# A graph layer on one core: 23 instead of 16 edge tiles whose rows SyncE fetches by byte address, a later range check, and another order of the last two groups

## The chip, the cores and the metric

The kernel runs on 1 core of a Trainium2 chip. The metric is the device time of one execution in microseconds. The median of three runs before the change is 1509.13 us (1508.41 to 1510.37).

## The reference

A message-passing layer over 6250 nodes and 200,000 edges, sorted by destination, followed by a residual and a layer norm over 64 features:

```python
w = silu(edge_attr @ W1 + b1) @ W2 + b2                        # 200000 x 9
h_src = features[src]                                          # one row of 64 per edge
msg = einsum('ef,em,fmg->eg', h_src, edge_sh * w, W_tp)
agg = segment_sum(msg, dst, num_segments=N) / sqrt(AVG_DEG)
emb = silu(c_noise[:, None] @ Wn1 + bn1) @ Wn2 + bn2
gamma, beta = split(emb, 2, axis=-1)
x = layernorm(x + agg * (1.0 + gamma) + beta)
```

## The kernel before

The edges are cut into 1563 tiles of 128, and 16 tiles make a group: 98 groups (`NBLK`), 0 to 97, the last with 11 tiles. The step `i` of the main loop works on several groups at once, and the order in which each engine gets its work is written out by hand (`tc.manual_schedule()`): an engine's instructions stand in its queue as the code emits them.

The rows `x[src]` of a group come into the tile `hs[g]` in three ways:
- `gather(g)` (L91): GpSimd's indirect DMAs, one per tile, issued six groups ahead (`AHEAD`) into seven buffers.
- `pick(g, t)` (L477): TensorE multiplies one-hot matrices `hot_k` (made by VectorE, in `hots`) with the whole of `x`, which lies in SBUF in two parts (`xs`), 14 products per tile into `px`; VectorE selects and sums the rows (`xm`, L486, and the reduction, L488). `picked(g)` says how many tiles of a group: four, three where `g % 4 == 0`, and three in group 97.
- `load_rows(g, e0)` (L101, L106): in the 16 groups of `SPG` (7, 13, ..., 97) SyncE fetches the rows of the group's first tile, each with a small DMA of its own. It loads up to 8 row numbers from `src_r` into registers, and each row's address is worked out from the register. `SPR` = 22 rows are issued per step, over six steps.

`src_r` is filled in the setup by one DMA of 2048 single words (L280).

SyncE's queue also holds the loads of edge attributes (`ea`, `sh`; one pair of groups every second step), of the keys for the picks (`kr`), of node values (`cb`), and the stores of the output.

In step `i` TensorE has, in this order: the first pick of group `i + 1` with small products for finished nodes among it (`nodes`), `hidden(i + 2)` (the first layer on edges, L405), `second(i + 1)` (its second layer into the PSUM tile `p2`, L422), `windows(i)` (L510: the rows of group `i` times the edge weights, 16 tiles, into `pz`; ScalarE copies the result to `zt`), in odd steps `project(i // 2)` (L550, with `W_tp`), and the other picks of group `i + 1`, with the transposes of `weights(i + 1)` in the first of them. `place` adds a pair of groups into node windows, `bring` turns finished nodes back, and `finish` and `finish_nodes` do the residual and the norm; the store is issued at the top of the next step.

`reach(k)`, in steps 3, 4 and 5, checks that the edges of each group lie in the range of nodes that the fast path takes: two reductions over 1568 columns on VectorE, then the limits (`bad`), a product on TensorE that counts (`p_bad`, L335), and the flag. It comes behind `hots(i + 2, 2, Q)` on VectorE and ahead of `hidden` on TensorE. `p_bad` and `p2` take turns in one PSUM buffer (tag `s`). At the end every engine reads the flag, and would run `general_path` if it were not zero.

Step 96 and what follows the loop are written out for the last groups: `windows(96)`, the picks of group 97 with `project(48)` and `place(48)` among them, `bring` of nodes 46 and 47, `windows(97)`, `project(49)`, and the last nodes.

Of the kernel before, what the change touches and what calls it, by code (L numbers as in the profile page):

```python
# [6 lines left out]

F32 = mybir.dt.float32
I32 = mybir.dt.int32
F16 = mybir.dt.float16  # L10
# [17 lines left out]
LB = 2  # L28
Q = 4
J = 7  # L30
SPG = range(7, NBLK, 6)
SPR = 22
EPS = 1e-5

KH = 8
# [9 lines left out]
def pair(q):  # L45

    return [g for g in (2 * q - 1, 2 * q) if 0 <= g < NBLK]


def picked(g):  # L50

    return Q - (g % 4 == 0 or g == NBLK - 1)


def tiles(g):
# [4 lines left out]
def gnn_resnorm_kernel(ctx: ExitStack, tc: tile.TileContext, x, src, dst, dst_row, ea, sh, cn,  # L60
# [18 lines left out]
    with ExitStack() as fast:  # L79
# [16 lines left out]
        src_r = keep.tile([len(SPG), P], I32)  # L96

        def load_rows(g, e0):
            for e in range(e0, min(e0 + SPR, P), 8):
                n = min(8, min(e0 + SPR, P) - e)  # L100
                _, vs = nc.values_load_multi_w_load_instructions(  # L101
                    src_r[SPG.index(g):SPG.index(g) + 1, e:e + n], engines=[mybir.EngineType.SP],
                    min_val=0, max_val=NPAD - 1,
                    skip_runtime_bounds_check_because="src is below N, as for the gathers")
                for k in range(n):
                    nc.sync.dma_start(hs[g][e + k:e + k + 1, 0, :], x[bass.ds(vs[k], 1), :])  # L106

        ident = keep.tile([P, P], F32)
        ident2 = keep.tile([P, F], F32)
# [11 lines left out]
        nid = keep.tile([P, NBLK], F32)  # L121
        first_f = keep.tile([KB, NBLK], F32)
        bad = keep.tile([P, 4], F32)
        ext = keep.tile([P, 4], F32)
        C = NBLK * Q
        jl = keep.tile([P, C], F32)
# [8 lines left out]
        def setup(temp):  # L135
# [143 lines left out]
            with nc.allow_non_contiguous_dma(reason="2048 words, once"):  # L279
                nc.sync.dma_start(src_r, src[:, SPG[0] * KB:NBLK * KB:6 * KB].rearrange("p g -> g p"))  # L280
            first_t = temp.tile([NBLK, KB], F32)
            nc.scalar.copy(first_t, first_i)
            p_f = psum.tile([KB, NBLK], F32, tag="s", name="p_f")
# [37 lines left out]
        def reach(k):  # L321

            if k < 2:
                nc.vector.tensor_reduce(ext[:, k:k + 1], rel, AX.X, (ALU.max, ALU.min)[k])
                return
            at = late.tile([KB, NBLK], F32, tag="at", name="at", bufs=1)
            nc.vector.tensor_sub(at, first_f, lo[0:KB])
            nc.vector.memset(bad, 0.0)
            for i, op in enumerate((ALU.max, ALU.min)):
                nc.vector.tensor_reduce(ext[0:KB, 2 + i:3 + i], at, AX.X, op)  # L330
            for i, (n, lim, op) in enumerate(((P, W - 0.5, ALU.is_gt), (P, -0.5, ALU.is_lt),
                                              (KB, 2 * P - W + 0.5, ALU.is_gt), (KB, -0.5, ALU.is_lt))):
                nc.vector.tensor_scalar(bad[0:n, i:i + 1], ext[0:n, i:i + 1], lim, None, op0=op)
            p_bad = psum.tile([1, 4], F32, tag="s", name="p_bad")
            nc.tensor.matmul(p_bad, nf[:, 1:2], bad, start=True, stop=True)  # L335
# [21 lines left out]

        stores = []

        def finish(j0, j1, sums):  # L360
            y = late.tile([P, j1 - j0, F], F32, tag="y", name=f"y{j0}")
            o = finish_nodes(nc, late, eps, sums, y, gam[:, j0:j1, :], xb[:, j0:j1, :], j0)
            stores.append(lambda: nc.sync.dma_start(out_v[:, j0:j1, :], o))


        ea_t, sh_t, oh_t, kr_t, st, a, zs = {}, {}, {}, {}, {}, {}, {}
# [126 lines left out]
                nc.vector.memset(z[:, :, tiles(g):, :], 0.0)  # L493
            return z

        def windows(g):

            nk = tiles(g)
            hsg, ag = hs.pop(g), a.pop(g)
            z = zs[g] if g in zs else sums(g)  # L500


            end = g == NBLK - 1
            for k0 in reversed(range(0, nk, ZT)) if end else range(0, nk, ZT):
                n = min(ZT, nk - k0)
                pz = [psum.tile([P, ZT // 2, M, W], F32, tag="pz", name=f"pz{g}_{k0}", bufs=2)]
                pz.append(psum.tile([P, ZT // 2, M, W], F32, tag="px", name=f"pz{g}_{k0}_", bufs=2) if end else pz[0])
                for k in range(n):
                    v = k % 2
                    mm = nc.tensor.matmul(pz[v][v * F:(v + 1) * F, k // 2].rearrange("p m w -> p (m w)"),  # L510
                                          hsg[:, k0 + k, :], ag[:, k0 + k].rearrange("p m w -> p (m w)"),
                                          start=True, stop=True)
                    if k0 + k == 0:

                        for d in hs_dma.pop(g)[(g not in SPG):]:
                            tc.add_manual_dep(mm.ins, d.ins.name, mybir.DependencyInfo(
                                mybir.DependencyClass.Sync, mybir.DependencyReason.DATA), reason="rows of the group")
                for v in range(2):
                    for h in range(2):
                        (nc.vector.tensor_copy if end and v else nc.scalar.copy)(  # L520
                            z[h * F:(h + 1) * F, 0:5 - h, k0 + v:k0 + n:2, :].rearrange("p m k w -> p k m w"),
                            pz[v][v * F:(v + 1) * F, 0:(n + 1 - v) // 2, h:M:2, :])

# [2 lines left out]
        def halves(q, pr):  # L526

            n = len(pair(q))
            r[q] = work.tile([KW, 2, 2, F], F32R, tag="r", name=f"r{q}")
            nc.scalar.copy(r[q][:, 0:n, 0], pr)  # L530
            nc.vector.tensor_sub(r[q][:, 0:n, 1], pr, r[q][:, 0:n, 0].bitcast(F32))
            for g in pair(q):
                hot[g] = work.tile([KW, 2 * P], F32R, tag="c", name=f"c{g}")
                nc.vector.tensor_scalar(hot[g], nf[0:KW], nid[0:KW, g:g + 1], None, op0=ALU.is_equal)

# [40 lines left out]

            return [lambda k=k: part(k) for k in range(len(gs))]

        def bring(j0, j1, py):


            def part(j):
                nc.tensor.matmul(py[:, j - j0], yt.pop(j), ident2, start=True, stop=True)
                if j == j1 - 1:
                    finish(j0, j1, py[:, 0:j1 - j0])

            return [lambda j=j: part(j) for j in range(j0, j1)]

# [18 lines left out]
        with tc.manual_schedule(), tc.tile_pool(name="temp", bufs=1) as temp:  # L607
            setup(temp)

            for i in range(NBLK):  # L610
# [26 lines left out]
                if i + 1 < NBLK:  # L637
                    second(i + 1)
                if i < NBLK - 1:
                    windows(i)  # L640
                turn = project(i // 2) if i % 2 == 1 and i < NBLK - 1 else []
                if i % 4 == 1 and i - 1 < NJ:
                    gate_hidden(i - 1)
                if i + 1 < NBLK:
                    pick(i + 1, 1, [weights(i + 1), turn])
                if i == NBLK - 2:
                    sums(i + 1)
                    turn = project(i // 2)
                    ps = psum.tile([P, 2 * P], F32, tag="s", name="ps_l")
                    pick(i + 1, 2, [turn])  # L650
                    more = place(i // 2, ps)
                    if picked(i + 1) < Q:
                        for f in more:
                            f()
                        more = []
                    pick(i + 1, 3, [more])
                    continue
                for t in range(2, Q):
                    pick(i + 1, t)
            for f in bring(NJ - 3, NJ - 1, psum.tile([P, FB, F], F32, tag="s", name="py_l")):  # L660
                f()
            windows(NBLK - 1)
# [15 lines left out]
def finish_nodes(nc, work, eps, sums, y, gam, xb, tag):  # L678
# [12 lines left out]
    nc.scalar.activation(var, var, AF.Sqrt, bias=eps, scale=1.0 / F)  # L691
    nc.vector.reciprocal(var, var)
    o = work.tile([P, n, F], F32, tag="o", name=f"o{tag}")
    nc.vector.tensor_mul(o, y, var.unsqueeze(2).to_broadcast([P, n, F]))
    return o


def general_path(tc, dram, x, dst_row, ea, sh, src_i, dst_i, w1bd, b1c, w2bd, b2r, wtc,
# [3 lines left out]
    with ExitStack() as ctx:  # L702
# [109 lines left out]
        for j0 in range(0, NJ, JC):  # L812
# [7 lines left out]
            o = finish_nodes(nc, work, eps, a[0], a[0], gam[:, js, :], xb[:, js, :], f"g{j0}")  # L820
            nc.sync.dma_start(out_v[:, js, :], o)


# [47 lines left out]
```

## Time and profile before

| | |
|---|---|
| median of three runs | 1509.13 us (1508.41 to 1510.37) |
| profiled execution | 1511.72 us, span 1509.5 us |
| mean granted TensorE clock | 0.985 |
| TensorE products | 1450.0 us busy, 96% |
| VectorE | 1149.6 us busy, 76% |
| GpSimd | 1124.0 us busy, 74% |
| ScalarE | 514.4 us busy, 34% |
| rows fetched by SyncE | 2048 DMAs of 256 bytes |
| gathers by GpSimd | 1181 |

The span runs from the first to the last instruction of the profiled execution. A line of the groups names the source line, the engine, the operation, output and inputs, the count, then busy time and mean duration in ns, then the engine's idle time before these instructions and what ended it. A line of the waits has total time, count and the longest in us. A line of the timeline has start, duration, engine, line and operation, and in brackets the idle time before it. PE is TensorE, DVE is VectorE, ACT is ScalarE, POOL is GpSimd, SP is SyncE; a "q" behind a name means the engine's queue.

### The profile page before, as it was taken

How to read it: one execution, taken by the hardware profiler on the slowest of the kernel's cores; microseconds unless marked ns; L12 is line 12 of the kernel's file. 1: busy time of each engine (PE TensorE's matmuls, PEld its weight loads, DVE VectorE, ACT ScalarE, POOL GpSimd, SP SyncE). 2: the span in 40 equal slices, each digit the busy share in tenths (PEclk: the TensorE clock that was granted, in tenths of full speed). 3: DMA queues.
4: the chain of work that ended last, by engine and by line, in shares of the span. 5: the costliest groups of instructions: out<-in, count | busy, mean ns of one | idle time of the engine just before them, and what ended most of it. 6: DMA issues, size and time to landing. Idle time of an engine off the chain costs nothing.

```text
span 1509.5 us, 34713 instructions
## 1 busy us (share of the span) xinstructions
PE 1450.0 (96%) x10969; PEld 1206.6 (80%) x10969; DVE 1149.6 (76%) x2043; ACT 514.4 (34%) x1321; POOL 1124.0 (74%) x1190
## 2 busy tenths in 40 slices
PE   5898999999999999999999999999999999999995
PEld 3687888887888888887888888888888888888784
DVE  6776777878777778787787777777787886877773
ACT  3322333423332424333333324233243342333331
POOL 7777777777777777777777777777777777777773
PEclk8899999999999999999999999999999999999997
DMA  5422222222222222222222222222222222222210
GB/s 166 95 74 63 55 59 71 61 61 72 58 63 55 75 53 66 57 72 58 60 72 54 60 54 72 54 61 70 55 62 53 72 56 58 73 54 60 59 42 17
DMA packets 90953, 96.34 MB, mean 64 GB/s; under 512 B 37224, under 2 KB 51770, under 8 KB 90762
## 3 DMA queue, kind: packets, MB, share of 16 engines
q1 hardware_dynamic: 52394, 53.66, 12.4%
q0 software_dynamic: 37792, 38.77, 11.6%
q8 instruction: 89, 1.46, 0.4%
q10 hardware_dynamic: 576, 1.61, 0.3%
q14 instruction: 102, 0.84, 0.2%
HBM read 92.22 MB, written 1.73 MB: 62 GB/s over the span
## 4 chain that ended last, share of the span: by engine, by line
PE 66%; POOL 17%; issue 7%; DVE 4%; DMA 3%; ACT 2%; SPq 0%; POOLq 0%; DVEq 0%; ACTq 0%
PE px L477 50%; POOL hs L91 17%; PE pz L510 5%; PE p L405 4%; DMA hs<-in_x_dram,src_i 3%; PE pt L550 3%; PE p L422 2%; PE p L432 1%; ACT L413 1%; ACT st L413 1%; PE ps L566 1%; DVE xm L486 1%; PE ps L596 1%; DVE hs L488 0%; DVE y L686 0%
## 5 line engine op out<-in xcount | busy, mean ns | idle before, releaser
L91 POOL DMA_INDIRECT hs<-in_x_dram,src_i x1181 | 1122.7, 951 | 362.0 <-issue 328.5
L477 PE MATMUL px<-xs,hot_k 128*128 128x448 f32 x5124 | 1124.7, 373 | 2.7 <-ACT xs L235 1.3
L477 PEld LDWEIGHTS px<-xs,hot_k 128*128 128x128 f32 x5124 | 926.7, 189 | 87.1 <-DVE xs L236 3.5
L486 DVE SCALAR_TENSOR_TENSOR xm<-li,jl,px 128x448 f32<-128x448 f32 x366 | 247.5, 676 | 221.8 <-PE px L477 221.6
L462 DVE TENSOR_TENSOR hot_k<-pk,nk 128x896 fp32r<-128x896 f32 x366 | 381.7, 1081 | 2.9 <-PE pk L221 2.9
L413 ACT ACTIVATE st<-p,b1c 128x1024 f32<-128x1024 f32 x98 | 109.2, 1114 | 401.0 <-PE p L405 400.7
L488 DVE TENSOR_REDUCE hs<-xm 128x64 f32<-128x448 f32 x366 | 226.9, 620 | 12.6
L520 ACT COPY ztw<-pz 64x140 f32<-64x140 f32 (+1 forms) x780 | 209.1, 268 | 14.6 <-PE pz L510 5.8
L510 PEld LDWEIGHTS pz<-a,hs 128*64 128x64 f32 x3116 | 100.5, 139 | 48.2 <-issue 46.9
L510 PE MATMUL pz<-a,hs 128*64 128x63 f32 x3116 | 113.8, 226 | 7.4 <-DMA hs<-in_x_dram,src_i 6.2
L444 DVE TENSOR_TENSOR a<-oh,p 128x1008 f32<-128x1008 f32 x98 | 117.9, 1203 | 3.3
L405 PE MATMUL p<-ea,w1bd 64*128 64x512 f32 x392 | 112.5, 651 | 0.0
L572 ACT COPY carry<-ps 128x128 f32<-128x128 f32 x48 | 12.8, 266 | 274.1 <-PE ps L566 274.1
L438 DVE TENSOR_TENSOR p<-p,sh 128x72 f32<-128x72 f32 x196 | 46.9, 240 | 69.7 <-PE p L432 39.6
L422 PEld LDWEIGHTS p<-st,w2p 128*32 128x32 f32 x784 | 15.8, 108 | 86.8 <-issue 44.6
L691 ACT ACTIVATE var<-var,eps 128x2 f32<-128x2 f32 (+1 forms) x25 | 7.4, 296 | 208.3 <-DVE var L690 208.3
L422 PE MATMUL p<-st,w2p 128*32 128x256 f32 x784 | 63.4, 395 | 12.2 <-DVE xb L354 7.6
L550 PE MATMUL pt<-ztw,wtc 128*64 128x112 f32 x960 | 55.9, 263 | 2.8 <-ACT st L413 2.8
L456 ACT CAST pk<-kr 128x512 f32<-128x512 f16 (+1 forms) x96 | 54.0, 562 | 1.7 <-DMA kr<-kd 1.7
L432 PE MATMUL p<-ident,p2s 128*128 128x128 f32 x196 | 53.6, 273 | 0.0
L405 PEld LDWEIGHTS p<-ea,w1bd 64*128 64x128 f32 x392 | 29.9, 187 | 29.0 <-issue 27.2
L550 PEld LDWEIGHTS pt<-ztw,wtc 128*64 128x64 f32 x960 | 47.1, 138 | 4.8 <-ACT st L413 4.5
(133 smaller groups left out, 525.8 us busy)
## 6 DMA issues: line engine op xcount, KB each, us to landing
hs<-in_x_dram SPq DMA_DIRECT2D x2048, 0.2 KB
ea<-in_ea_dram SPq DMA_DIRECT2D x48, 512.0 KB
hs<-in_x_dram,src_i POOLq DMA_INDIRECT x1181
kr<-kd SPq DMA_DIRECT2D x48, 256.0 KB
sh<-in_sh_dram SPq DMA_DIRECT2D x49, 144.0 KB
cb<-cn_d SPq DMA_DIRECT2D x12, 128.0 KB
out_dram<-o SPq DMA_DIRECT2D x24, 64.0 KB
dst_i<-in_dst_dram SPq DMA_DIRECT2D x1, 768.0 KB
```

The source lines that it names most:

```text
L91: hs_dma[g] = [nc.gpsimd.indirect_dma_start(out=hs[g][:, t - g * KB, :], out_offset=None, in_=x, in_offset=bass.IndirectOffsetOnAxis(ap=sr ...
L405: nc.tensor.matmul(p1[:, i, :], w1bd[i * 64:(i + 1) * 64, :], e[i * 64:(i + 1) * 64, :], start=True, stop=True)
L413: nc.scalar.activation(st[g], p1_t.pop(g), AF.Silu, bias=b1c)
L422: nc.tensor.matmul(p2[g][c * D:(c + 1) * D, 0, :].rearrange("p (i e) -> p i e", i=2), w2p, s[:, :, c * P:(c + 1) * P], start=True, stop=True)
L444: nc.vector.tensor_mul(a[g], oh_t.pop(g)[:, :, None, :].to_broadcast([P, KB, M, W]), sw.unsqueeze(3).to_broadcast([P, KB, M, W]))
L462: nc.vector.tensor_tensor(hot_k[g, t], pk_t[g][:, t, None, :].to_broadcast([P, J, P]), nk.unsqueeze(2).to_broadcast([P, J, P]), op=ALU.is_ ...
L477: nc.tensor.matmul(px.rearrange("p f l -> p (f l)"), hot_k[g, t][:, h, :], xs[i][:, h].rearrange("p f l -> p (f l)"), start=(h == 0 and i ...
L486: nc.vector.scalar_tensor_tensor(xm, li[:, None, :].to_broadcast([P, F, J]), jl[:, c:c + 1], px, op0=ALU.is_equal, op1=ALU.mult)
L488: nc.vector.tensor_reduce(hs[g][:, tiles(g) - q + t, :], xm, AX.X, ALU.add)
L510: mm = nc.tensor.matmul(pz[v][v * F:(v + 1) * F, k // 2].rearrange("p m w -> p (m w)"), hsg[:, k0 + k, :], ag[:, k0 + k].rearrange("p m w ...
L520: (nc.vector.tensor_copy if end and v else nc.scalar.copy)(z[h * F:(h + 1) * F, 0:5 - h, k0 + v:k0 + n:2, :].rearrange("p m k w -> p k m w ...
L550: nc.tensor.matmul(pt[h * F:(h + 1) * F, 0, 0:KW], wtc2[:, c, :], z[h][:, c], start=(c == 0), stop=(c == 4))
```

## The change

It does five things.
1. `SPG` becomes 7, 11, ..., 95: 23 groups. Each is fetched in four steps of 32 rows (`SPS`, `SPR`), three steps earlier than it would have to be. Group 97 is no longer among them.
2. The row numbers are multiplied by 256 and transposed on TensorE in the setup (`row_f`, `p_row`, `row_a`) instead of loaded by a DMA of single words. SyncE loads 32 registers at a time, and the row's DMA takes the byte address from the register as it is, with `x` and the row of `hs` seen as bytes.
3. The range check runs in steps 56 to 58, and its last part (`reach_all`: `p_bad`, the count, the flag) in step 60.
4. Group 97 has four picks.
5. The loop ends in step 96 after its first pick. The rest stands in another order: `windows(96)` behind two more picks, the last pick, `project(48)`, `windows(97)` in two halves with `place(48)` and `bring` between them. The Sqrt of the norm is used once early on a spare value; for nodes 46 and 47 the part of the norm from the Sqrt on is emitted behind the second half of `windows(97)`, and ScalarE alone copies that group's results.

The core of the diff:

```diff
-SPG = range(7, NBLK, 6)
-SPR = 22
+SPS = 4
+SPG = range(7, NBLK, SPS)
+SPR = P // SPS
...
-    return Q - (g % 4 == 0 or g == NBLK - 1)
+    return Q - (g % 4 == 0)
...
-            for e in range(e0, min(e0 + SPR, P), 8):
-                n = min(8, min(e0 + SPR, P) - e)
+            for e in range(e0, e0 + SPR, 32):
+                n = min(32, e0 + SPR - e)
...
-                    nc.sync.dma_start(hs[g][e + k:e + k + 1, 0, :], x[bass.ds(vs[k], 1), :])
+                    nc.sync.dma_start(hs[g][e + k:e + k + 1, 0, :].bitcast(U8), x8[bass.ds(vs[k], 4 * F)].unsqueeze(0))
...
-                nc.sync.dma_start(src_r, src[:, SPG[0] * KB:NBLK * KB:6 * KB].rearrange("p g -> g p"))
+            row_f = temp.tile([P, len(SPG)], F32)
+            nc.vector.tensor_scalar(row_f, src_i[:, SPG[0] * KB:NBLK * KB:SPS * KB], 4.0 * F, None, op0=ALU.mult)
+            p_row = psum.tile([len(SPG), P], F32, tag="s", name="p_row")
+            nc.tensor.transpose(p_row, row_f, ident)
+            nc.vector.tensor_copy(row_a, p_row)
...
-                    if 0 < g - i <= AHEAD:
+                    if AHEAD - SPS < g - i <= AHEAD:
                         load_rows(g, (AHEAD - g + i) * SPR)
...
-                if 3 <= i <= 5:
-                    reach(i - 3)
+                if 56 <= i <= 58:
+                    reach(i - 56)
+                if i == 60:
+                    reach_all()
...
+            g = NBLK - 1
+            second(g)
+            nc.scalar.activation(spare, eps, AF.Sqrt)
+            pick(g, 1, [weights(g)])
+            pick(g, 2)
+            sums(g)
+            windows(g - 1)
+            pick(g, 3)
+            marks(g // 2)
+            turn = project(g // 2)
+            windows(g, [ZT])
+            ends = []
+            for f in turn + place(g // 2, psum.tile([P, 2 * P], F32, tag="s", name="ps_l")):
+                f()
+            marks(NBLK // 2)
+            for f in bring(NJ - 3, NJ - 1, psum.tile([P, FB, F], F32, tag="s", name="py_l"), ends):
+                f()
+            windows(g, [0])
+            ends.pop()()
+            project(NBLK // 2)
```

`marks(q)` is the part of `halves` that makes the one-hot matrices `hot` for `place`, so that it can be emitted earlier.

More of the change, by code (lines that the diff above doesn't have):

```diff
@@ L9 @@
 I32 = mybir.dt.int32
+U8 = mybir.dt.uint8
 F16 = mybir.dt.float16
@@ L94, in gather @@
                 for t in range(g * KB + (g in SPG), g * KB + tiles(g) - picked(g))]
-        src_r = keep.tile([len(SPG), P], I32)
+        row_a = keep.tile([len(SPG), P], I32)
+        x8 = x.bitcast(U8).rearrange("n c -> (n c)")
         def load_rows(g, e0):
-            for e in range(e0, min(e0 + SPR, P), 8):
-                n = min(8, min(e0 + SPR, P) - e)
+            for e in range(e0, e0 + SPR, 32):
+                n = min(32, e0 + SPR - e)
                 _, vs = nc.values_load_multi_w_load_instructions(
-                    src_r[SPG.index(g):SPG.index(g) + 1, e:e + n], engines=[mybir.EngineType.SP],
-                    min_val=0, max_val=NPAD - 1,
+                    row_a[SPG.index(g):SPG.index(g) + 1, e:e + n], engines=[mybir.EngineType.SP],
+                    min_val=0, max_val=4 * F * (NPAD - 1),
                     skip_runtime_bounds_check_because="src is below N, as for the gathers")
                 for k in range(n):
-                    nc.sync.dma_start(hs[g][e + k:e + k + 1, 0, :], x[bass.ds(vs[k], 1), :])
+                    nc.sync.dma_start(hs[g][e + k:e + k + 1, 0, :].bitcast(U8), x8[bass.ds(vs[k], 4 * F)].unsqueeze(0))
         ident = keep.tile([P, P], F32)
@@ L123, in gnn_resnorm_kernel @@
         bad = keep.tile([P, 4], F32)
+        spare = keep.tile([P, 1], F32)
         ext = keep.tile([P, 4], F32)
@@ L278, in setup @@
             nc.sync.dma_start(wn2a[H:H + 1, :], bn2.unsqueeze(0))
-            with nc.allow_non_contiguous_dma(reason="2048 words, once"):
-                nc.sync.dma_start(src_r, src[:, SPG[0] * KB:NBLK * KB:6 * KB].rearrange("p g -> g p"))
+            row_f = temp.tile([P, len(SPG)], F32)
[3 more added lines that the diff above has]
+            nc.vector.tensor_copy(row_a, p_row)
             first_t = temp.tile([NBLK, KB], F32)
@@ L333, in reach, with reach_all @@
                 nc.vector.tensor_scalar(bad[0:n, i:i + 1], ext[0:n, i:i + 1], lim, None, op0=op)
+        def reach_all():
             p_bad = psum.tile([1, 4], F32, tag="s", name="p_bad")
@@ L358, in gnn_resnorm_kernel, with finish, store @@
         stores = []
-        def finish(j0, j1, sums):
+        def finish(j0, j1, sums, parts=None):
             y = late.tile([P, j1 - j0, F], F32, tag="y", name=f"y{j0}")
-            o = finish_nodes(nc, late, eps, sums, y, gam[:, j0:j1, :], xb[:, j0:j1, :], j0)
-            stores.append(lambda: nc.sync.dma_start(out_v[:, j0:j1, :], o))
+            end = finish_nodes(nc, late, eps, sums, y, gam[:, j0:j1, :], xb[:, j0:j1, :], j0)
+            def store():
+                o = end()
+                stores.append(lambda: nc.sync.dma_start(out_v[:, j0:j1, :], o))
+            if parts is None:
+                store()
+            else:
+                parts.append(store)
         ea_t, sh_t, oh_t, kr_t, st, a, zs = {}, {}, {}, {}, {}, {}, {}
@@ L494, in sums, with windows @@
             return z
-        def windows(g):
+        def windows(g, k0s=None):
             nk = tiles(g)
-            hsg, ag = hs.pop(g), a.pop(g)
+            end = g == NBLK - 1
+            hsg, ag = hs[g], a[g]
             z = zs[g] if g in zs else sums(g)
-            end = g == NBLK - 1
-            for k0 in reversed(range(0, nk, ZT)) if end else range(0, nk, ZT):
+            for k0 in range(0, nk, ZT) if k0s is None else k0s:
                 n = min(ZT, nk - k0)
@@ L519, in windows @@
                     for h in range(2):
-                        (nc.vector.tensor_copy if end and v else nc.scalar.copy)(
+                        nc.scalar.copy(
                             z[h * F:(h + 1) * F, 0:5 - h, k0 + v:k0 + n:2, :].rearrange("p m k w -> p k m w"),
@@ L531, in halves, with marks @@
             nc.vector.tensor_sub(r[q][:, 0:n, 1], pr, r[q][:, 0:n, 0].bitcast(F32))
+            marks(q)
+        def marks(q):
             for g in pair(q):
+                if g in hot:
+                    continue
                 hot[g] = work.tile([KW, 2 * P], F32R, tag="c", name=f"c{g}")
@@ L577, in place, with bring @@
             return [lambda k=k: part(k) for k in range(len(gs))]
-        def bring(j0, j1, py):
+        def bring(j0, j1, py, ends=None):
             def part(j):
@@ L584, in part @@
                 if j == j1 - 1:
-                    finish(j0, j1, py[:, 0:j1 - j0])
+                    finish(j0, j1, py[:, 0:j1 - j0], ends)
             return [lambda j=j: part(j) for j in range(j0, j1)]
@@ L632, in gnn_resnorm_kernel @@
                     hots(i + 2, 2, Q)
-                if 3 <= i <= 5:
-                    reach(i - 3)
+                if 56 <= i <= 58:
+                    reach(i - 56)
+                if i == 60:
+                    reach_all()
                 if i + 2 < NBLK:
                     hidden(i + 2)
[L637 to L641, printed above, removed]
+                if i == NBLK - 2:
+                    break
+                second(i + 1)
+                windows(i)
+                turn = project(i // 2) if i % 2 == 1 else []
                 if i % 4 == 1 and i - 1 < NJ:
                     gate_hidden(i - 1)
[L644 to L657, printed above, removed]
+                pick(i + 1, 1, [weights(i + 1), turn])
                 for t in range(2, Q):
                     pick(i + 1, t)
-            for f in bring(NJ - 3, NJ - 1, psum.tile([P, FB, F], F32, tag="s", name="py_l")):
-                f()
-            windows(NBLK - 1)
+            g = NBLK - 1
[11 more added lines that the diff above has]
+            for f in turn + place(g // 2, psum.tile([P, 2 * P], F32, tag="s", name="ps_l")):
+                f()
+            marks(NBLK // 2)
[3 more added lines that the diff above has]
+            ends.pop()()
             project(NBLK // 2)
@@ L690, in finish_nodes, with end @@
     nc.vector.tensor_reduce(var, sq, AX.X, ALU.add)
[L691 to L695, printed above, removed]
+    def end():
+        nc.scalar.activation(var, var, AF.Sqrt, bias=eps, scale=1.0 / F)
+        nc.vector.reciprocal(var, var)
+        o = work.tile([P, n, F], F32, tag="o", name=f"o{tag}")
+        nc.vector.tensor_mul(o, y, var.unsqueeze(2).to_broadcast([P, n, F]))
+        return o
+    return end
 def general_path(tc, dram, x, dst_row, ea, sh, src_i, dst_i, w1bd, b1c, w2bd, b2r, wtc,
@@ L819, in general_path @@
             nc.vector.tensor_add(a[0], a[0], a[2])
-            o = finish_nodes(nc, work, eps, a[0], a[0], gam[:, js, :], xb[:, js, :], f"g{j0}")
+            o = finish_nodes(nc, work, eps, a[0], a[0], gam[:, js, :], xb[:, js, :], f"g{j0}")()
             nc.sync.dma_start(out_v[:, js, :], o)
```

## The prediction

> **What bounds the kernel now.** I read the page first, then who waited for whom, then the timeline at the places where TensorE stood still, and last SyncE's queue line by line.
>
> ```profile
> L91 POOL DMA_INDIRECT hs<-in_x_dram,src_i x1181 | 1122.7, 951 | 362.0 <-issue 328.5
> L477 PE MATMUL px<-xs,hot_k 128*128 128x448 f32 x5124 | 1124.7, 373 | 2.7 <-ACT xs L235 1.3
> ```
>
> Two engines run from end to end. GpSimd has 951 ns per gather and 0.30 us of issue behind each: 1.2515 us, and 1181 of them are 1478 us. TensorE is busy 1450 of 1509.5 us. Who is last shows in the waits:
>
> ```profile
> PE p_bad L335 <- DVE bad L333: 4.8, 1, 4.8
> PE pz L510 <- DMA hs<-in_x_dram,src_i: 6.2, 5, 3.8
> ```
>
> Until group 87 a gathered group lies ready when `windows` takes it: 38 us early at group 7, 2.5 to 5 us early near 90. From group 88 on TensorE waits for rows. Windows of groups 88, 89, 92 and 93 start 0.45, 0.31, 1.56 and 0.44 us later than the same step of a four-step cycle before them, 2.76 us in all, and the last wait is the longest:
>
> ```profile
> 1479.65 1.53 PE L510 MATMUL pz<-a,hs 128*64 128x63 f32 x32 [3.85 <-DMA hs<-in_x_dram,src_i]
> 1481.11 1.12 PE L477 MATMUL px<-xs,hot_k 128*128 128x448 f32 x2
> ...
> 129.54 0.19 PE L335 MATMUL p_bad<-bad,nf 128*1 128x4 f32 x2 [4.80 <-DVE bad L333]
> 129.66 2.08 PE L405 MATMUL p<-ea,w1bd 64*128 64x512 f32 x4
> ```
>
> So the kernel is TensorE's chain with GpSimd exactly abreast at the end: TensorE's time is worth something only if gathers are removed too, and the change does both.
>
> **The skill on a standing TensorE.** The Trainium skill, "TensorE: Matmul & The Clock Gate", section "Part 1: The HAM clock gate", says that about 3.4 us of idle halve TensorE's clock, and that about as long of work restores it. The trace agrees: PEclk is 0.51 from 128.5 to 135.4 after the 4.80 us wait, 0.50 from 1480.2 to 1483.6 after the 3.85 us one, and a pair of products takes 1.12 us instead of 0.65. A 1.48 us wait at 1418 left the clock alone. So I count a wait above 3 us at its length plus about 2 us. For `p_bad`: groups 3 to 6 start windows at 98.4 and 149.8, 51.4 us, the same three steps twelve groups later 43.7 us: **7.7 us**.
>
> **SyncE's rows.** Per row the queue holds a register multiplication, a move and a DMA:
>
> ```profile
> L106 SPq FUSED_REGOPS  x2048: 37/37/51, 64.0 to 1475.4; - x187
> L106 SPq MOVE hs<-in_x_dram x2048: 29/29/43, 64.4 to 1475.4; - x187
> L106 SPq DMA_DIRECT2D hs<-in_x_dram x2048: 224/228/312, 64.5 to 1475.5; - x187
> 729.30 0.64 SPq L106 DMA_DIRECT2D hs<-in_x_dram  x2
> L101 SPq TENSOR_LOAD <-src_r x1: 725/725/725, 596.3 to 596.3; - x1
> L101 SPq TENSOR_LOAD <-src_r x1: 979/979/979, 605.3 to 605.3; - x1
> L101 SPq TENSOR_LOAD <-src_r x1: 1882/1882/1882, 609.8 to 609.8; - x1
> ```
>
> Two rows in 0.64 us less the last DMA's 0.228 are 0.412 us a row. With byte addresses the multiplication goes (37 ns and 35 ns to the next): **0.34 us**. The three loads are of 8, 6 and 8 registers, from words 0, 16 and 22 of a row. The skill, "Runtime: NRT & Kernel Launch", section "Instruction fetch mechanics", gives about 200 ns per register. The row at 609.8 agrees (1.88 us for 8), and so do 1.54 us for 6 and 0.72 us for 2 from odd places: 0.2 us each over 0.3 us. But words that start at a multiple of four (16 bytes) take 0.73 us for 8 and 0.98 for 6, so four come in one read of about 0.24 us. The new loads start at words 0, 32, 64, 96: 0.27 + 8 x 0.24 = **2.2 us**. I go by the trace; the page's rule would give 6.4 us, and I keep that as the end of the range.
>
> Per four steps SyncE then needs 128 x 0.34 = 43.5, four loads with their gaps and slower first rows 4 x 2.4 = 9.6, the other DMAs (ea and sh twice, kr twice, cb, out) 4.1 and 0.7 for the pauses of 0.35 us that its queue shows every 27 us: 57.9 us, 57.4 once `cb` has ended. TensorE's cycle is 59.5 us (windows 14 to 18) and later 58.2 (66 to 70). SyncE keeps up with about 1 us to spare. Today it waits some 3 us per cycle for the out store, and `ea` is issued 12 us before `hidden` with 4 us to landing: 8 us more of lead.
>
> **Part by part.**
> 1. 23 tiles instead of 16 lie with SyncE. Group 97 was one of them and is none now, so 15 + 1 become 23 + 0; in 97 the fourth pick replaces a gather. Gathers: 1181 - 8 = 1173, GpSimd ends 8 x 1.25 = 10.0 us earlier, 8.8 us earlier at group 92. The rows of group 92 are then there at 1409.4 instead of 1418.1. The 2.76 us of waits go, if TensorE isn't faster by more than this; then the rows cap it.
> 2. Setup: the 2048-word DMA (0.63 us of SyncE's queue) goes; a product, two small DVE instructions (some 0.2 us each) and a wait for them come, while TensorE and DVE wait for `first_t` until 44.4 anyhow. Without that cover 0.5 us. Counted 0. SyncE's rows start 1 to 2 us earlier, useful: `ea` of group 6 is issued only 4.7 us before its use.
> 3. Range check: the 7.7 us at step 5 go. At steps 56 to 58 its reductions (1.78, 1.77, 1 us of DVE) lie where steps 3 and 4 show no TensorE stall from them: 0. But in step 60 `p_bad` and the next `p2` share one PSUM buffer, and `p2` waits for `n_bad`, which stands on DVE behind two `hot_k`:
>
> ```profile
> 949.52 0.64 PE L422 MATMUL p<-st,w2p 128*32 128x256 f32 x8
> 949.96 0.62 DVE L488 TENSOR_REDUCE hs<-xm 128x64 f32<-128x448 f32 x1
> 950.49 2.08 DVE L462 TENSOR_TENSOR hot_k<-pk,nk 128x896 fp32r<-128x896 f32 x2
> ```
>
> These `hot_k` end at 952.6; TensorE, 0.2 us of `p_bad` later than here, stands from 949.7 to 952.75: 3.05 us, and windows, projection and picks queue behind it. With the clock 4.9 us (3.05 to 6.5). None of these moves issues a DMA, so no queue of SyncE or GpSimd is passed. Net gain **2.8 us**.
> 4. Tail, from `second(97)`'s start (1475.16 before) to the last `o` (1503.56): 28.4 us. After: 0.6 `p2`; pick 1 with transposes 3.2; pick 2 2.9; windows(96) 1.15 (its rows, at 1469.7, are early now); pick 3 2.9; project 1.15; then DVE's `xm` and reduction of pick 3 end 1.3 us after the pick, the 3 windows 0.3: 12.2. ACT copies and the cast of `r` 1.25, sub 0.3, place 0.5, yt 0.3, bring 0.7, the 8 windows 0.4: 15.7. ACT's four copies 1.1, project 2.1 (half clock, as at 1496.36), cast to yt 1.4, bring 0.75, the nine instructions to `o` 2.5: 23.6. The node pair's finish (2.3 us of DVE) and the Sqrt table load (1.28) now lie under these. Gain **4.8 us**, with one pick (2.9) more.
>
> Sum: 2.8 + 2.8 + 4.8 = 10.4 us. The profiled execution took 1511.72 us (span 1509.5, 2.2 around it), so 1501.3 for it; the median stands 2.6 below: **1498.8 us**.
>
> **Rivals.**
> (a) SyncE becomes the bound, and the kernel is slower. Place: 32 rows plus a load in each of 92 steps. It decides once a cycle needs more than 58.2 (late) or 59.5 us (early) by more than its 8 us of lead allow. At 0.36 us a row and 2.6 us a load with gaps it needs 61.2: 2.2 x 11.5 + 3 x 11.5 - 8 = 52 us, 1541 us with the gains above. At 6.4 us a load it is 74 us and over 1800 us in all. For it: the spare is 1 us in 58. Against: the 0.34 is a sum of measured pieces, and the aligned loads are consistent over every row.
> (b) The stall at step 60 costs as much as the old one (6.5 us) and the tail gains 2: 2.8 + 1.2 + 2 = 6 us, 1503 us. For it: the idle clock windows in the tail.
> (c) The stall at step 60 is small. Then the gathers cap TensorE (rows of 92 at 1409.4): 3.3 us more, 1495.5 us.
> (d) Nothing comes of it: SyncE drifts behind by a little and eats the 10 us (a cycle of 59.5 late, 1.3 x 11.5 - 8 = 7, early 0): 1506 to 1509 us.
>
> **Chances.** My forecast with (c): 0.62; (b) 0.13; (d) 0.09; (a) 0.16. About 0.2% (3 us) is what a measurement of this kernel can tell from no change: faster 0.75, same 0.08, slower 0.17. The range runs from the cap of (c), 1494.5, over (b) and (d) to 1512; beyond it lie most of (a) and little else. The likely cases alone span 1495 to 1503.
>
> **What would show it.** Right: no wait of `pz` for gathered rows; rows 0.34 us apart, loads near 2.2 us; a stall of 3 us at `p2` of group 61 with half clock; none in step 5; some 23.6 us from `second(97)` to `o`. Wrong: TensorE waiting for `ea` or `kr`, loads above 2.7 us, or rows above 0.36 us.

## The result and the profile after

The changed kernel takes 1517.03 us (median of 5 runs, 1516.59 to 1518.18) against 1509.13 us before: ratio 1.0054, 95% interval 1.0039 to 1.0069. It is slower by 8 us where 10 us less were forecast. Its profiled execution has a span of 1516.3 us, against 1509.5.

From the page of the kernel after, the groups of GpSimd's gathers and of the one-hot products (count, then busy time and mean ns of one):

```profile
L93 POOL DMA_INDIRECT hs<-in_x_dram,src_i x1173 | 1111.8, 948 | 359.6 <-issue 320.3
L494 PE MATMUL px<-xs,hot_k 128*128 128x448 f32 x5138 | 1141.7, 375 | 2.7 <-ACT xs L239 1.3
```

From its waits (total, times, longest):

```profile
PE p L439 <- DVE n_bad L346: 3.0, 1, 3.0
PE pz L527 <- DMA hs<-in_x_dram,src_i: 1.9, 7, 0.3
```

The wait for `bad` is gone, the one for gathered rows has shrunk from 6.2 to 1.9 us in pieces of at most 0.3, none of them in groups 88 to 96, and the new wait for `n_bad` is 3.0 us. So the waits went as they should. But the products are busy for 17.0 us more, although only the 14 products of one pick were added (2.8 us). The timeline shows where that lies: one and the same stretch of 34 products with nothing between them, in the kernel before

```profile
1027.08 7.06 PE L477 MATMUL px<-xs,hot_k 128*128 128x448 f32 x34
```

and in the kernel after:

```profile
1034.74 7.18 PE L494 MATMUL px<-xs,hot_k 128*128 128x448 f32 x34
```

0.12 us over 34 products is 3.5 ns for each. From start to start, two products with no other work between them are 200.7 ns apart before and 204.0 after. This distance in time is called the spacing below (means of the 4115 and 4133 such steps under 220 ns; before, most of them are exactly 200 ns, after they go round 196, 200, 203, 209 and 212). 4133 steps of 3.3 ns are 13.8 us. It is there from the first groups on, before SyncE issues its first row at 64 us.

SyncE's queue (duration in ns, shortest/median/longest) did as expected: loads of 32 registers in 2.1 us, and its rows 0.323 us apart.

```profile
L104 SPq TENSOR_LOAD <-row_a x92: 2047/2110/2368, 62.0 to 1415.0; - x92
L109 SPq DMA_DIRECT2D hs<-in_x_dram x2944: 227/228/309, 64.5 to 1428.0; - x197
```

In the experiments a, b, c, e and g1 below, the kernel before, run beside them, itself took 2419 to 2525 us, with all engines standing at times; of those only the spacing of products and the order of waits is read, not the time (one and the same kernel had the ratio 0.978 there as a1 and 1.010 as c1).

### The profile page after: what moved, and what is told of

The parts are those of the page before. It is cut to its first block, busy times and chain, and to the rows that moved or that the text cites. A ratio compares the mean times of both kernels' runs of the same rounds, so it can differ in the third digit from the quotient of the medians.

```text
span 1516.3 us, 34381 instructions
## 1 busy us (share of the span) xinstructions
PE 1465.4 (97%) x10984; PEld 1207.4 (80%) x10984; DVE 1151.0 (76%) x2044; ACT 514.3 (34%) x1326; POOL 1113.1 (73%) x1182
## 4 chain that ended last, share of the span: by engine, by line
PE 73%; POOL 9%; DVE 5%; issue 5%; DMA 3%; ACT 3%; SPq 2%; POOLq 0%; DVEq 0%; ACTq 0%
PE px L494 55%; POOL hs L93 9%; PE pz L527 5%; PE p L422 4%; DMA hs<-in_x_dram,src_i 3%; PE pt L573 3%; PE p L439 3%; SPq L109 1%; PE p L449 1%; ACT L430 1%; ACT st L430 1%; DVE xm L503 1%; DVE hs L505 1%; PE ps L589 1%; PE ps L619 0%
## 5 line engine op out<-in xcount | busy, mean ns | idle before, releaser
L494 PE MATMUL px<-xs,hot_k 128*128 128x448 f32 x5138 | 1141.7, 375 | 2.7 <-ACT xs L239 1.3
L442 ACT ACTIVATE p2s<-p,b2c 128x256 f32<-128x256 f32 x98 | 45.7, 467 | 15.7 <-PE p L439 15.7
```

What stands on the lines that cost most here:

```text
L494: nc.tensor.matmul(px.rearrange("p f l -> p (f l)"), hot_k[g, t][:, h, :], xs[i][:, h].rearrange("p f l -> p (f l)"), start=(h == 0 and i ...
```

## The experiments

One row of the diff had no part in the forecast: `spare = keep.tile([P, 1], F32)`, 4 bytes per partition in the pool `keep`, ahead of everything that is laid out later. In the built programs it takes 32 bytes, so `hot_k` starts at byte 189088 of a partition and not at 189056, while `xs` stays at 138784. All steps between slices and buffers of `xs` and `hot_k` (1792, 12544, 512 and 3584 bytes) are multiples of 256, so every product of a kernel has the same distance from its `xs` to its `hot_k`, modulo 256: 96 before, 128 after.

Theory L: the place of the tiles slows the products. Theory S: SyncE's longer loads and more rows do, or another part of the change. From L came theory R: what counts is the distance between `hot_k` and `xs`.

### The tile alone, out and in: a1, b1, a2, b2

a1, the kernel after with `spare` as a fifth column of `bad` (the memset and the counting product keep to the first four):

```diff
-        bad = keep.tile([P, 4], F32)
-        spare = keep.tile([P, 1], F32)
+        bad = keep.tile([P, 5], F32)
+        spare = bad[:, 4:5]
```

> The changed kernel with the spare value in a fifth column of the tile bad, so that no tile behind it in SBUF moves: hot_k begins at a multiple of 64 bytes again, as in the kernel before. Theory L (the 32 bytes of the spare tile moved hot_k, and each of 5138 products takes 204.0 ns from start to start instead of 200.7): products back at 200.7 ns, 5138 x 3.3 ns = 17 us less, median 1499 to 1502 us. Theory S (the denser row DMAs of SyncE or another part of the change slow the products): still 204 ns, 1516 to 1518 us.

b1, the kernel before with an unused tile of 4 bytes; a2, the kernel after with a second one:

```diff
         bad = keep.tile([P, 4], F32)
+        gap = keep.tile([P, 1], F32)
+        nc.vector.memset(gap, 0.0)
```

> The kernel before with one unused 4-byte tile where the change has its spare tile; nothing else. Theory L: products at 204 ns, 17 us more of TensorE, of which up to 8 us come out of the waits for gathered rows at the end, so 1517 to 1526 us. Theory S: 1509 us as before, products 200.7 ns.

> The changed kernel with a second unused 4-byte tile behind the spare one, so that hot_k lies 64 bytes and not 32 behind its old place. If the place within 64 bytes counts (theory L): 200.7 ns and 1499 to 1502 us. If any move of hot_k counts, or theory S holds: 204 ns and 1516 to 1518 us.

b2, the kernel before with `hot_k` where it was and `xs` 32 bytes lower, so at the distance 128:

```diff
-        b2c = keep.tile([P, 1], F32)
         xs = [keep.tile([P, J, F, J], F32R, name=f"xs{i}") for i in range(2)]
+        b2c = keep.tile([P, 1], F32)
```

> The kernel before with the small tile b2c placed behind xs, so that both tiles xs (the moving operand of the picks) begin at a multiple of 64 bytes, and hot_k (the weights) stays on one. If each operand off a 64-byte line costs by itself: products under 200.7 ns, but the gathers of GpSimd cap the time, 1500 to 1508 us. If it is the two operands in the same half of a line that cost (in the changed kernel both lie at 32): about 204 ns, 1517 to 1526 us. If the moving operand's place does not count: 1509 us.

Measured, mean spacing: a1 201.9 ns with the commonest step back at 200; b1 203.8; a2 205.3; b2 203.7. The kernel before has 201.5 ns in such a long execution (e2, below), so a1 is back at its pace. b1 has nothing of the change but the tile, and has the pattern of the kernel after: S falls. a2 does not return to 200, so a rule of 64-byte places for `hot_k` falls too. b2 has the pattern of after with `hot_k` unmoved: neither operand's own address decides, their distance explains all four. That is R.

### Seven distances in one run: c2, e3

c2 and e3 are a1 with each of the seven buffers of `hot_k` 32 bytes longer:

```diff
-hot_k[g, t] = late.tile([P, J, P], F32R, tag="hot_k", name=f"hot_k{g}_{t}", bufs=7)
+hk = late.tile([P, J * P + 8], F32R, tag="hot_k", name=f"hot_k{g}_{t}", bufs=7)
+hot_k[g, t] = hk[:, 0:J * P].rearrange("p (h e) -> p h e", h=J)
```

> The kernel of c1_spare_inside with each of the seven hot_k buffers 32 bytes longer, so that the seven lie 96, 128, 160, 192, 224, 0 and 32 bytes past xs0 modulo 256. Theory R: the spacing differs by buffer within this one run: 200.7 ns in the buffer at 96, 204.0 at 128, 205.3 at 160, the others unknown. Theory A (what counts is another tile's address, or the layout as a whole, not hot_k against xs): all seven buffers have one spacing. The time is no test; the mean spacing over the seven says it, about 1500 to 1525 us.

> The kernel of c2_scan again: seven hot_k buffers at 96, 128, 160, 192, 224, 0 and 32 bytes past xs0 modulo 256. Theory R: mean spacings by buffer as in c2_scan, 200.7, 204.0, 205.3, 200.6, 204.5, 202.9 and 204.4 ns, each within 0.4.

Mean spacing by buffer, in ns, some 450 to 500 steps each:

```text
distance modulo 256     96    128    160    192    224      0     32
c2                   201.2  204.0  205.3  200.6  204.5  202.9  204.4
e3                   201.3  203.8  205.3  200.6  204.5  202.9  204.1
```

R predicted three of these from other kernels (96 from before, 128 from b1, 160 from a2), to 0.6 ns, within one kernel in which everything else is equal. The kernel before happened to lie on one of the two good places.

### What it is worth in time: c1, c3, d1, d3, e4

c1 and d1 are a1's kernel again, c3 and d3 are b1's. e4 mends the kernel after in another way, with a larger tile:

```diff
-        spare = keep.tile([P, 1], F32)
+        spare_w = keep.tile([P, 17], F32)
+        spare = spare_w[:, 0:1]
```

> Made to differ from the changed kernel by one thing: `spare` is a fifth column of `bad`, so hot_k lies 96 bytes past xs0 modulo 256 as before, not 128. Theory R (the distance of hot_k from xs sets the pace of the one-hot products): mean spacing 200.7 ns as before, so 5124 x 3.3 ns = 17 us less than the changed kernel's 1517.0: 1499 to 1502 us, which is 7 to 10 us faster than before. Rival S (SyncE's reads or rows, or another part of the change, slow the products): spacing 204, 1516 to 1518 us.

> The kernel before with an unused 4-byte tile where the change puts `spare`, and nothing else of the change. Theory R: spacing 203.8 ns, 5124 x 3.1 ns = 16 us slower than before: 1522 to 1527 us. Rival S (the change's other parts slow the products): no difference, 1508 to 1511 us.

> The changed kernel with one edit: `spare` is a column of a tile of 68 bytes in place of 4, so hot_k lies 192 bytes past xs0 modulo 256, not 128. Theory R: spacing 200.6 ns and the time of d1_spare_inside, 1504 to 1505.5 us, against 1517.0 of the changed kernel. Rival D (d1's gain came from there being no tile of its own for `spare`): 1516 to 1518 us.

c1 had 201.4 ns, c3 203.9 and e4 200.5; their times say nothing, so what e4 gains in time stays untested. d1 and d3 gave times:

> The kernel of c1_spare_inside again: hot_k 96 bytes past xs0 modulo 256 as before, everything else as changed. Theory R: spacing 200.7 ns, about 17 us less than the changed kernel's 1517.0: 1499 to 1502 us, against 1509.1 before. Rival S (another part of the change slows the products): 1516 to 1518 us.

> The kernel before with the unused 4-byte tile that lays hot_k 128 bytes past xs0 modulo 256. Theory R: spacing 203.9 ns, 5124 x 3.2 ns = 16 us above before: 1522 to 1527 us. Rival S: 1508 to 1511 us.

d1: 1504.69 us (8 runs), ratio 0.9972 (0.9962 to 0.9983), spacing 200.7. d3: 1518.24 us (4 runs), ratio 1.0056 (1.0040 to 1.0073), spacing 204.0. The kernel before took 1509.07 us beside them. Both have the sign that R gives, and both are smaller than I expected. The same 34 products, first in d1, then in d3:

```profile
1025.09 7.06 PE L494 MATMUL px<-xs,hot_k 128*128 128x448 f32 x34
```

```profile
1037.49 7.18 PE L479 MATMUL px<-xs,hot_k 128*128 128x448 f32 x34
```

The expectations had taken 3.3 ns for all 5124 products. Between d1 and after the uninterrupted steps make 829.9 us against 843.1 (4136 and 4133 of them), and the 533 steps from a product to another instruction 219.9 ns against 222.7 each: 13.2 + 1.5 = 14.7 us. The steps of 220 to 600 ns, some 470, kept their 300 ns. The spans differ by 13.8, since after's setup was 1.1 us longer, its step 60 1.5 us cheaper (below) and its tail 0.4 us shorter. In d3 the 4600th product starts 13.8 us later than in the kernel before, but the last instruction ends only 7.0 us later: TensorE's waits for gathered rows, 6.2 us before, have shrunk to this:

```profile
PE pz L512 <- DMA hs<-in_x_dram,src_i: 0.4, 1, 0.4
```

A slower TensorE first uses up its own wait for GpSimd. The changed kernel has taken that wait away already, so there the loss counts in full.

### The range check in step 60: c4, d2

```diff
-                if i == 60:
-                    reach_all()
...
                 for t in range(2, Q):
+                    if i == 60 and t == 3:
+                        reach_all()
                     pick(i + 1, t)
```

on a1's kernel.

> The kernel of c1_spare_inside with reach_all (the range check's product, n_bad, the flag) moved within step 60 from ahead of second(61) to between the third and the fourth pick of that step. Theory W (the 2.95 us wait of second(61) for n_bad is on the path): 2.5 to 3.2 us less than c1_spare_inside, 1496 to 1499 us. Rival (n_bad stops something later on TensorE or GpSimd, or the wait was cover for another): within 0.5 us of c1_spare_inside.

> The kernel of d1_spare_inside with reach_all between the third and fourth pick of step 60. Theory W: no wait of second(61) for n_bad, and 2.5 to 3.2 us less than d1_spare_inside: 1496 to 1499 us. Rival: the wait of 2.95 us only stood where another would have been, within 0.5 us of d1_spare_inside.

c4's time can't be read, though the wait for `n_bad` is gone in its trace. d2: 1500.08 us (4 runs), ratio 0.9944 (0.9927 to 0.9960), 4.6 us under d1: more than the 3.2 us I allowed for. The timeline of step 60 in d1, then in d2:

```profile
941.89 1.13 PE L422 MATMUL p<-ea,w1bd 64*128 64x512 f32 x4
946.00 0.64 PE L439 MATMUL p<-st,w2p 128*32 128x256 f32 x8 [2.97 <-DVE n_bad L346]
946.57 1.76 PE L527 MATMUL pz<-a,hs 128*64 128x63 f32 x32
```

```profile
941.59 1.13 PE L422 MATMUL p<-ea,w1bd 64*128 64x512 f32 x4
942.64 0.64 PE L439 MATMUL p<-st,w2p 128*32 128x256 f32 x8
943.21 1.15 PE L527 MATMUL pz<-a,hs 128*64 128x63 f32 x32
```

The windows take 1.76 us in d1 and 1.15 in d2: the clock. In d1's table by stretches the column after the engines' busy times is PEclk:

```profile
946.00:948.00 2.00, 2.00 (x38) 1.59 (x40) 0.12 (x1) 0.95 (x3) 1.39 (x3) 0.71 0.32 82
948.00:950.00 2.00, 2.00 (x12) 1.65 (x10) 0.00 (x0) 1.92 (x8) 1.70 (x2) 0.50 0.16 33
950.00:952.00 2.00, 2.00 (x11) 1.76 (x10) 1.35 (x3) 0.23 (x1) 1.39 (x3) 0.93 0.12 21
```

Between the 3200th and the 3400th product d1 loses 4.7 us against the kernel before, d2 0.3. Theory W holds, with the clock's part on top. In the kernel after the same wait, 2.95 us long, left the clock alone:

```profile
956.33 0.64 PE L439 MATMUL p<-st,w2p 128*32 128x256 f32 x8 [2.95 <-DVE n_bad L346]
956.89 1.15 PE L527 MATMUL pz<-a,hs 128*64 128x63 f32 x32
```

The Trainium skill, "TensorE: Matmul & The Clock Gate", section "Part 1: The HAM clock gate", calls the activity window of about 3.4 us free-running, so that the moment of a change depends on where in it the work falls. This pair fits: 2.97 us brought half clock, 2.95 us did not. In each of the seven traces of normal length (before, after, d1 to d4, f1) all changes of the clock lie whole multiples of 3.41 us apart. Cut into such intervals, 2.56 us of d1's wait fall into one of them (TensorE is busy for 0.86 of its 3.42 us), and the next interval has half clock:

```profile
943.44:946.86 3.42, 0.86 (x18) 0.45 (x20) 2.65 (x5) 0.90 (x2) 2.51 (x4) 1.00 0.34 97
946.86:950.27 3.41, 3.41 (x37) 2.92 (x33) 0.00 (x0) 2.94 (x10) 2.53 (x3) 0.50 0.15 29
```

In after the wait is split over two intervals, 1.29 and 1.66 us, and the clock stays:

```profile
951.25:954.66 3.41, 2.12 (x11) 0.93 (x9) 3.38 (x5) 1.11 (x1) 2.50 (x4) 1.00 0.12 26
954.66:958.07 3.41, 1.75 (x41) 1.27 (x41) 1.75 (x4) 0.91 (x3) 2.63 (x3) 1.00 0.40 106
```

So it counts where a wait lies among these intervals, and not only how long it is. How much standing in one interval halves the clock, these traces don't settle.

### SyncE's tiles as before: d4

```diff
-SPS = 4
+SPS = 6
 SPG = range(7, NBLK, SPS)
-SPR = P // SPS
+SPR = 22
```

on a1's kernel, with the bounds of `load_rows` cut at `P`.

> The kernel of d1_spare_inside with SyncE taking the first tile of every sixth group in parts of 22 rows, as before, in place of every fourth in parts of 32 (addresses still in bytes, by TensorE's transpose). Theory G (the extra seven tiles take GpSimd off the path in the last groups): the waits of TensorE for gathered rows in the windows of groups 88 to 93 come back, 2.8 us more than d1_spare_inside. Rival (those windows wait for nothing once the rest has changed): within 0.5 us of it.

d4: 1505.54 us (15 runs), ratio 0.9981 (0.9973 to 0.9989); in the profiled spans 0.6 us above d1. Neither side has it. The wait for gathered rows did come back, at group 92:

```profile
1415.56 1.15 PE L527 MATMUL pz<-a,hs 128*64 128x63 f32 x32 [2.07 <-DMA hs<-in_x_dram,src_i]
```

By the 5060th product, from the 4600th on, d1 gains 2.1 us on d4 by that; d4's step 60 also costs 1.7 us more (half clock for longer), its tail 1.0 us less. But up to the 2600th d1 had lost 2.2 us to d4. They lie in front of the windows of groups 7, 11, 15 and so on to 47: TensorE stands there for 0.24 to 0.28 us in all eleven of them, in d4 only in 7, 19, 31 and 43. Group 11, in d1 and in d4:

```profile
215.96 0.64 PE L439 MATMUL p<-st,w2p 128*32 128x256 f32 x8 [0.69 <-DVE xb L363]
216.88 1.15 PE L527 MATMUL pz<-a,hs 128*64 128x63 f32 x32 [0.28 <-issue]
```

```profile
215.99 0.64 PE L439 MATMUL p<-st,w2p 128*32 128x256 f32 x8 [0.80 <-DVE xb L363]
216.56 1.15 PE L527 MATMUL pz<-a,hs 128*64 128x63 f32 x32
```

These are the groups with rows from SyncE. The wait shows only in steps in which TensorE has just waited for `xb`, one in four up to step 47; and every fourth group is now a SyncE group, on just these steps.

### SyncE's groups off those steps: e1, f1, g1

d2's kernel with `SPG = range(6, NBLK, SPS)` (e1, f1) or `range(10, NBLK, SPS)` (g1).

> The kernel of d2_check_later with SPG = range(6, NBLK, SPS): SyncE brings the first tile of groups 6, 10, 14 and so on, not 7, 11, 15. Theory X (the 0.26 us ahead of the windows show only where a group with SyncE's rows falls on the steps i = 3 modulo 4 up to 47, in which TensorE has just waited for the end of `finish`): the eleven waits go, 2 to 3 us less than d2_check_later's 1500.1: 1497 to 1498.5 us. Rival (the wait goes with SyncE's rows wherever they are): 1499.5 to 1501 us.

> The kernel of d2_check_later with SPG = range(6, NBLK, SPS), as e1_groups_from_six. Theory X: the waits of 0.26 us ahead of the windows of groups 7 to 47 go with their coincidence with the steps i = 3 modulo 4, 2 to 3 us less than d2_check_later: 1497 to 1498.5 us, or 0.992 to 0.993 of before. Rival (other steps pay the same): 1499.5 to 1501 us, 0.9935 to 0.995 of before.

e1 had none of these waits, but no time to read. f1: 1507.21 us (15 runs), ratio 0.9981 (0.9974 to 0.9989): 7 us worse than d2 (5.6 us by the ratios, since the kernel before stood at 1510.64 us beside f1), where 2 to 3 us better was expected. Theory X is right nevertheless: none of the eleven waits is left, and from the 400th to the 2600th product f1 gains 3.5 us on d2. It lost 10.6 us ahead of the 200th. SyncE's queue there, and who waited:

```profile
75.42 10.28 SPq L109 DMA_DIRECT2D hs<-in_x_dram  x32
85.74 0.41 SPq L390 DMA_DIRECT2D ea<-in_ea_dram  x1
```

```profile
89.41 2.08 PE L422 MATMUL p<-ea,w1bd 64*128 64x512 f32 x4 [8.05 <-DMA ea<-in_ea_dram]
```

Group 6 has its rows issued from step 0 on, while SyncE is still behind from the setup; 32 of them stood ahead of `ea`, and TensorE waited 8.05 us. That is the mechanism of the forecast's rival (a) on a small scale: a row in SyncE's queue costs whoever waits for what is behind it.

> The kernel of d2_check_later with SPG = range(10, NBLK, SPS): SyncE brings the first tile of groups 10, 14 and so on up to 94, GpSimd that of group 6. Theory Y (the start and the eleven waits are separate costs): no wait for ea at 81 us, no wait ahead of the windows of groups 7 to 47, 3.0 to 3.5 us less than d2_check_later's 1500.1: 1496 to 1498 us, 0.991 to 0.993 of before. Rival (SyncE is late at the start wherever its first rows stand, the delay only comes later): about 1507 us, 0.998 of before.

g1 has no wait ahead of the windows of groups 7 to 47 either, but its time and its start can't be read. So a start at group 10 is untested; d2 less f1's 3.5 us would be 1496.6 us, an estimate.

### The kernel before once more: e2

> The kernel before, unchanged, for a second profiled execution. If the waits of the windows of groups 88 to 96 for gathered rows hold from one execution to the next, they again sum to about 6.2 us, and the span is 1509 to 1510 us. If they change with the execution, the sum differs by over 1 us and the span with it: 1506 to 1508 us with shorter waits.

Beside its spacing nothing can be told from it: the time was 2506 us, with waits everywhere. How long before's waits for gathered rows are in other executions stays open.

## Why the prediction was wrong

By its own terms, read from the starts of the same products in two traces, in us against the kernel before:

```text
term                                        forecast      d1     after
step 5, no wait for `bad`                       -7.7    -7.8      -7.8
step 60, wait for `n_bad` and clock             +4.9    +4.7      +3.2
gathered rows, groups 88 to 96                  -2.8    -2.7      -2.8
tail, second(97) to the last `o`                -4.8    -2.5      -2.9
SyncE's groups 7 to 47                             0    +2.1      +2.1
setup                                              0    -1.1      -0.1
distance of hot_k from xs                          0       0     +14.7
sum of the profiled spans (measured)           -10.4    -7.1      +6.8
```

The terms add up to -7.3 and +6.4; what is missing to the spans lies in single steps of 0.1 us. The 2.1 us of SyncE's groups are d1's against d4; after has the same eleven waits. The setup was 1.1 us shorter in d1, 0.9 to 1.4 in d2, d4 and f1, and not in after. That is the clock: TensorE had half of it from about 16 to 23 us in before, after and d3, and all of it from 18.6 us at the latest to 25 or later in the other four. Before and after, with the same clock there, differ by 0.1 us, which fits the forecast's 0; whether the change has a part in when the clock turns is not shown. First before, then d1:

```profile
19.70:22.70 3.00, 3.00 (x12) 2.83 (x12) 1.46 (x4) 0.00 (x0) 2.39 (x3) 0.50 0.78 270
19.70:22.70 3.00, 3.00 (x19) 2.79 (x19) 1.79 (x5) 0.12 (x1) 2.39 (x3) 1.00 0.76 259
```

**The step that failed** is in "Part by part": the pace of the 5124 products has no term there, so it was put at nothing without a reason. Every product's price, 200 ns (2.9 us a pick in point 4), was carried from the trace of before into another layout. In point 4 `spare` was only the early Sqrt, an instruction that lies under other work; that its tile moves `hot_k` was not looked at. No rival had it either. In its place the runs showed 204.0 ns for 200.7, which makes 14.7 us between d1 and after, and b1 and d3 show that the tile alone does it.

**Point 1 was right.** TensorE no longer waits for rows in groups 88 to 93; in d4 2.1 of the 2.8 us came back. What it lacked are the 0.26 us of TensorE in front of a SyncE group's windows: four such waits stood in the trace of before (groups 7, 19, 31, 43), and eleven came.

**SyncE was right**, and rivals (a) and (d) fell: rows 0.323 us apart (0.34 forecast), loads 2.1 us (2.2), and the waits of its queue for the out store rose from 49.6 to 122.7 us, so it has more time to spare, not less. That the loads follow the trace was the right choice: the 2.1 us are 66 ns a register, not the 200 ns of the Trainium skill, "Runtime: NRT & Kernel Launch", section "Instruction fetch mechanics". Only in f1, with rows in the first steps, was rival (a)'s mechanism seen. Rival (a)'s sum is wrong, though nothing hangs on it: 61.2 less 59.5 and 58.2 makes 1.7 and 3.0 us, so 46 us, not 52, and 1545 us in all, not 1541.

**Point 3 was right**: 7.8 us gone in step 5, a wait of 2.95 us for 3.05 at the place named. Whether the clock follows was not to be known from the wait's length alone: it did in d1, not in after. So d1's 4.7 us for 4.9 is in part luck.

**Point 4's size was off**: 25.5 us for 23.6, in d1 25.9. Before its `windows(97)` halves there is more standing than I summed. The first three windows end 0.7 us later than in the sum (its parts add up to 12.35, not 12.2), `place` and `bring` bring 0.3 more, and the eight windows run at half clock, 1.1 us for 0.4. It sets in at 1500.78, after an interval of 3.41 us in which TensorE stood for 1.95 us, 1.27 and 0.68 of them here:

```profile
1499.17 0.51 PE L589 MATMUL ps_l<-c,r 112*128 112x256 f32 x2 [1.27 <-DVE r L548]
1500.35 0.75 PE L606 MATMUL py_l<-ident,yt 128*128 128x64 f32 x4 [0.68 <-DVE yt L598]
1501.03 0.37 PE L527 MATMUL pz<-a,hs 128*64 128x63 f32 x1
```

**The step to the median failed too.** I took 2.6 us off because the profiled execution of before stood that far above its median, as though the changed kernel's would. After's stands 1.15 us above, d1's 0.4 below. Before's profiled span of 1509.5 us is longer than each of its 22 spans beside d1 (1503.8 to 1508.8), so a part of what the change takes away from it is not there in the usual execution; which part, the runs don't tell. d1 gains 7.1 us between the profiles and 4.4 between the medians.

With the distance as before, the forecast mechanism is in d1, at 42% of the gain (4.4 of 10.4 us; what is missing are mainly 2.3 us of the tail, 2.1 of SyncE's groups and the step to the median); with the check moved within step 60, d2 is the fastest measured version, 9 us below before.

## What to carry to other kernels

A new tile, however small, can move everything laid out after it: compare the addresses of the operands of the busiest instruction before and after an edit, and its start-to-start time in the trace before anything else. Price a slower instruction only on the steps that it sets alone, and first let it use up the waits of its own engine. A second price per use, such as 0.26 us ahead of a consumer, can hide in a trace until an edit lines its uses up with the steps in which the consumer has just waited for something else.

## What the runs showed of the hardware

- A product of 128x128 fp32r weights with a 448-column moving operand has a pace that depends on the distance between the two in SBUF: 200.6 to 205.3 ns over seven distances 32 bytes apart, with good places at 96 and 192 modulo 256. The Trainium skill, "SBUF — State Buffer", section "Operand start alignment", asks for element alignment and says that this is about legality, not speed; the runs show a speed. Why, no run tells. The period of 256 bytes comes from the steps of these tiles, and was not varied.
- Standing for 2.97 us halved TensorE's clock in one kernel, standing for 2.95 us in another did not: the clock changed only at whole intervals of 3.41 us, and one interval held 2.56 us of the first wait, but at most 1.66 us of the second. 1.95 us in one interval were followed by half clock at the end of after.
- Executions of one and the same kernel spread by 5 us in the span (before, 1503.8 to 1508.8 beside d1), more than most of the terms above.
